# Moving layer 1's first normalise, transpose and gate into the experts' second round

## The chip, the core and the metric

The kernel runs on one core of one Trainium2 chip. Its time is the device time in microseconds (us) of one execution; each figure given as a median is the median of several executions. The engines of the core are PE (TensorE, matrix products and transposes), DVE (VectorE), ACT (ScalarE), POOL (GpSimd) and SP (SyncE, which here only issues transfers). They run their own instruction queues in order and meet at semaphores.

## What is computed

The reference is a network of two layers over x of shape (2, 2048, 256). Cut to what matters here:

```
x = L0_attn_x
xn = layernorm(x)
s = linear_attention(xn)                     # layer 0
g = silu(block(xn))                          # softmax attention + mixture of 8 experts, top 2
x = x + s * g
xn = layernorm(x)                            # layer 1
s = softmax_attention(xn; Wq, Wk, Wv, Wo)    # 16 heads of 32, causal per 2048 tokens
g = silu(xn @ int4(kernel) + bias + (xn @ a) @ b)
x = x + s * g
```

The tokens lie in 32 tiles of 128, 16 tiles for each of the two batches. Layer 1 needs the finished `x` of layer 0, and so the output of the experts for each token.

## The kernel before, in words

**Layer 0's attention** runs first and ends at about 1443 us of the profile. What follows has two stages, and the change touches both and the border between them.

**The experts** (the loops over `h` and `e` from L1356 on). Each expert's 1024 slots are done in two rounds of 512: `h` = 0 for all eight experts, then `h` = 1. One pass of the inner loop loads the expert's weights, biases and slots (`xe`), transposes `xe` on PE (L1374), applies the norm's scale on DVE (`affine`, L1322), makes the hidden layer with 16 matmuls and a Gelu on ACT (L1380, L1381), then the output with 32 matmuls (L1386), adds the bias on DVE (`ye`, L1389) and writes `ye` to `slots_out` (L1391). This stage is written out in program order and a framework's scheduler places each engine's instructions.

Two generators advance between experts. `int4` (L1269) rounds the gate's weight `wl` to int4. `first_mix` is `early_mix` (L1327): for the first four tiles (tokens whose slots all lie in the first round) it gathers the experts' rows from `slots_out` (POOL, L1337), weighs and adds them (L1344 to L1346), applies the Silu (ACT, L1348), multiplies by `s` and adds x (L1349, L1350), and takes the norm's statistics (`norms`). It is advanced from the third expert of the second round on (L1394).

**Layer 1's attention** is written as steps on a list. `Plan` orders all steps of all engines with a search over a model of their costs, and the order that it finds is what each engine runs. `run_attention` (L529) first adds the parts that `prepare` (L1727) returns for the first head group, then interleaves two passes over blocks of the score matrix: pass a takes row maxima (L554 on PE, L567 and L573 on DVE), pass b forms the weights (L587, L1585, L520 on PE, the exponential L599 on ACT), sums them (POOL, L1597 to L1602) and multiplies by the values (L1620, L1631).

The parts for batch 0 go in chunks `c` of four tiles:
- `mix(n0)` for the tiles that `early_mix` has not done: load x and s (L1451, L1452), gather (POOL, L1459), weigh (ACT, L1468), add (DVE, L1473, L1474), Silu (ACT, L1439), multiply and add (L1481, L1482), statistics (DVE L491, L493; POOL L477 and its neighbours);
- `norm(G, t)` for two tiles: scale (ACT, L1501 into `hn`), transpose (PE, L372), copy to `xt` (ACT, L1508);
- `project`: queries and keys of the chunk (PE L1527, copies L1532 on ACT and L1534 on DVE) and values (PE L1542, copy L1548);
- `gate(0, c)`: the low-rank product (PE L1698, copied to `lt` by DVE at L1703), twelve matmuls with `wl` and `lb` (PE L1713, L1714), Silu (ACT L1720), and two writes to `g_dram` (SP, L1725), which `finish` reads at L1682.

`parts.insert` in `prepare` sets the order of these parts before the search. PSUM has eight banks in this stage, five `s` and two `t` banks in the experts' stage; `turn_pair` there takes a `t` bank.

Of the kernel before, what the change touches and what calls it, by code (L numbers as in the profile page):

```python
# [10 lines left out]
F32 = mybir.dt.float32  # L11
# [315 lines left out]
def kernel(ctx: ExitStack, tc: tile.TileContext, i: dict, out: bass.AP):  # L327
# [9 lines left out]
    def bank(tag="s"):  # L337
        return psum[0].tile([P, 512], F32, tag=tag, name=tag, bufs={"s": 5, "t": 2, "av": 1}[tag])
# [126 lines left out]
    def slots(pool, name, count, shape, dt=F32):  # L465
        return [
            lambda n=n: pool.tile(list(shape), dt, tag=f"{name}{n}", name=name, bufs=1) for n in range(count)
        ]
# [203 lines left out]
    with ExitStack() as sc:  # L672
# [70 lines left out]
        def norm(G, t):  # L743
            hn, tp = Buf("hn"), Buf("s")
            n0 = G.b * NT + t

            def shrink():
                for n in range(2):
                    nc.scalar.mul(hn.t[:, n], xr[:, n0 + n], ln_r1[:, n0 + n : n0 + n + 1])

            def scale():
                for k in range(2):
                    nc.vector.tensor_scalar(
                        ht[:, k, t * P : (t + 2) * P], tp.t[:, 2 * k * P : 2 * (k + 1) * P],
                        cols[:, k : k + 1], cols[:, 2 + k : 3 + k], ALU.mult, ALU.add,
                    )

            S("prep", "ACT", 0.75, shrink, r=[("xr", n0), ("xr", n0 + 1), r_of[n0]], w=[hn])
            S("prep", "PE", 0.45, lambda: turn_pair((hn.t[:, 0], hn.t[:, 1]), tp.t), r=[hn], w=[tp])
            S("prep", "DVE", 0.9, scale, r=[tp], w=[("ht", t), ("ht", t + 1)])  # L760
# [503 lines left out]
    for mpad in mpads1:  # L1264
        nc.gpsimd.memset(mpad, 0.0)
    lt = w.tile([17, 512], F32, name="lt")
    nc.gpsimd.memset(lt, 1.0)

    def int4_grid(pool):  # L1269
# [47 lines left out]
    with ExitStack() as sc:  # L1317
        wk = sc.enter_context(tc.tile_pool(name="moe", bufs=2))
        int4 = int4_grid(sc.enter_context(tc.tile_pool(name="int4", bufs=1)))

        def affine(dst, src, k):
            nc.vector.tensor_scalar(dst, src, cols[:, 4 + k : 5 + k], cols[:, 6 + k : 7 + k], ALU.mult, ALU.add)  # L1322

        after = mybir.DependencyInfo(mybir.DependencyClass.Sync, mybir.DependencyReason.DATA)
        w1_in = i["L0_ffn_W1"].rearrange("e (k p) f -> e p k f", p=P)
        w2_in = i["L0_ffn_W2"].rearrange("e (f p) n -> e p f n", p=P)
        def early_mix(n0, pool):  # L1327

            gx, xs = (pool.tile([P, 2, 4, D], F32, name=x) for x in ("early_g", "early_x"))
            x = xr[:, n0 : n0 + 4]
            nc.sync.dma_start(xs[:, 0], x_in[:, n0 : n0 + 4])
            nc.sync.dma_start(xs[:, 1], s_dram[:, n0 : n0 + 4])
            for n, (_, back, _) in enumerate(routes):
                for t in range(4):
                    nc.gpsimd.indirect_dma_start(  # L1337
                        out=gx[:, n, t], out_offset=None, in_=slots_out[: E * HALF],
                        in_offset=bass.IndirectOffsetOnAxis(ap=back[:, n0 + t : n0 + t + 1], axis=0),
                    )  # L1340
            yield
            for n, (_, _, m) in enumerate(routes):
                for t in range(4):
                    nc.vector.tensor_scalar_mul(gx[:, n, t], gx[:, n, t], m[:, n0 + t : n0 + t + 1])  # L1344
            nc.vector.tensor_tensor(gx[:, 0], gx[:, 0], gx[:, 1], ALU.add)
            nc.vector.tensor_tensor(gx[:, 0], gx[:, 0], x, ALU.add)  # L1346
            yield
            nc.scalar.activation(gx[:, 0], gx[:, 0], AF.Silu)  # L1348
            nc.vector.tensor_tensor(gx[:, 0], gx[:, 0], xs[:, 1], ALU.mult)  # L1349
            nc.vector.tensor_tensor(x, gx[:, 0], xs[:, 0], ALU.add)  # L1350
            yield
            norms(pool, lambda strand, eng, cost, fn, **_: fn())("", n0, "", ln_r, ln_m)

        first_mix = early_mix(0, sc.enter_context(tc.tile_pool(name="early", bufs=1)))

        for h in range(2):  # L1356
            for e in range(E):
                w1, w2 = carried[e % 2].rearrange("p (k f) -> p k f", k=2), carried[2 + e % 2].rearrange("p (f n) -> p f n", n=D)
                nc.sync.dma_start(w1, w1_in[e])
                nc.sync.dma_start(w2, w2_in[e])  # L1360
                b2 = wk.tile([P, D], F32, name="b2")
                nc.sync.dma_start(b2, i["L0_ffn_b2"][e : e + 1, :].to_broadcast([P, D]))
                r0 = e * CAP + h * HALF
                xe = wk.tile([P, 4, D], F32, name="xe")
                load = nc.sync.dma_start(xe, slots_in[r0 : r0 + HALF, :].rearrange("(s p) d -> p s d", p=P))
                for inst in sent if e == h == 0 else ():
                    tc.add_manual_dep(load.ins, inst.name, after, reason="every token is in its place")
                if e == h == 0:
                    load_l1()
                xt = wk.tile([P, 2, 512], F32, name="xt")  # L1370
                for k in range(2):
                    tp = bank("t")
                    for s in range(4):
                        nc.tensor.transpose(tp[:, s * P : (s + 1) * P], xe[:, s, k * P : (k + 1) * P], ident)  # L1374
                    affine(xt[:, k], tp, k)
                hm = wk.tile([P, FF // P, 512], F32, name="hm")
                for f in range(FF // P):
                    ps = bank()
                    for k in range(2):
                        nc.tensor.matmul(ps, w1[:, k, f * P : (f + 1) * P], xt[:, k], start=k == 0, stop=k == 1)  # L1380
                    nc.scalar.activation(hm[:, f], ps, AF.Gelu, bias=b1c[:, e * 8 + f : e * 8 + f + 1])  # L1381
                ye = wk.tile([P, 4, D], F32, name="ye")
                for s in range(4):
                    ps = bank()
                    for f in range(FF // P):
                        nc.tensor.matmul(  # L1386
                            ps[:, :D], hm[:, f, s * P : (s + 1) * P], w2[:, f], start=f == 0, stop=f == FF // P - 1
                        )
                    nc.vector.tensor_tensor(ye[:, s], ps[:, :D], b2, ALU.add)  # L1389
                out0 = (h * E + e) * HALF  # L1390
                nc.sync.dma_start(slots_out[out0 : out0 + HALF, :].rearrange("(s p) d -> p s d", p=P), ye)  # L1391
                if e or h:
                    next(int4, None)
                if h and e > 1:  # L1394
                    next(first_mix, None)
        for _ in int4:
            pass
    ps_moe.close()


# [1 line left out]

    g_dram = dram.tile([P, NA, D], F32, name="g_dram")
    with ExitStack() as sc:
        wk = sc.enter_context(tc.tile_pool(name="l1", bufs=2))
        ps = sc.enter_context(tc.tile_pool(name="ps_l1", bufs=1, space=bass.MemoryType.PSUM))
# [3 lines left out]
                **held, vt=slots(wk, "vt", 2, [P, NT, 4, 32]),  # L1412
                mx=slots(wk, "mx", 2, [P, 2, 4, 4]), pt=slots(wk, "pt", 5, [P, 4, 512]), ps=slots(wk, "ps", 2, [P, 4, QC]),
                hn=slots(w, "hn", 1, [P, 2, D]), wg=slots(w, "wg", 1, [P, 3, 2, P]),
                xt=slots(w, "xt", 1, [P, 2, T]), m=slots(wk, "m", 2, [P, 2, 4]),
                mhalf=slots(wk, "mhalf", 2, [P, 2, 2, 4], BF16), mh=slots(wk, "mh", 3, [P, 512], BF16),
                un=slots(wk, "un", 3, [P, 512]), oc=slots(wk, "oc", 2, [P, QC]),
                rs=slots(wk, "rs", 2, [P, 8, 1]), rw=slots(wk, "rw", 1, [P, 8, 32]),
# [12 lines left out]
        def mix(n0, of=2):  # L1431

            both = [(n0 + n, Buf("gx"), Buf("xs")) for n in range(0, of, 2)]
            for n0, gx, xs in both:
                fetched(n0, gx, xs)

            def silus():
                for _, gx, _ in both:
                    nc.scalar.activation(gx.t[:, 0], gx.t[:, 0], AF.Silu)  # L1439

            got = [gx for _, gx, _ in both]
            S("mix", "ACT", 1.4 + 0.6 * len(both), silus, r=got, w=got)
            for n0, gx, xs in both:
                mixed(n0, gx, xs)
# [282 lines left out]
        def prepare(G):  # L1727
            parts = []
            project(G, parts)
            if G.g == 0:  # L1730
                for c in range(NT // 4):
                    for t in (0, 2):
                        parts.insert(5 * c + t // 2, lambda t=4 * c + t: norm(G, t))
            if G.b == G.g == 0:
                for c in range(NT // 4):
                    for t in (0, 2) if c else ():
                        parts.insert(8 * c - 2 + t // 2, lambda n0=4 * c + t: mix(n0))
                    parts.insert(8 * c + 2, lambda c=c: gate(0, c))
            return parts

        others = [(24 + 16 * n, lambda n0=NT + 4 * n: mix(n0, 4)) for n in range(NT // 4)]
# [33 lines left out]
```

## Time and profile before

| what | value |
|---|---|
| median of 3 runs | 3442.45 us (3442.42 to 3448.39) |
| the profiled execution | 3434.15 us, span 3432.4 us from first to last instruction |
| last expert's last bias add ends | about 1920.3 us |
| PE busy, first round of experts (1443 to 1676 us) | 229.67 of 233 us |
| PE busy, second round (1676 to 1920 us) | 232.58 of 244 us |
| PE busy, 1920 to 2010 us | 79.61 of 90 us, mean granted clock 0.87 |
| PE busy, 2100 to 2450 us | 338.18 of 350 us |
| PE busy, 2450 to 3325 us | 867.99 of 875 us |
| PE busy, 3325 to 3432 us | 95.86 of 107 us |

Times inside the execution are counted from the start of the span. The rows of PE come from the profile's windows: the busy time of each engine in a stretch, and the mean clock that the throttle granted to TensorE there (1.00 is full speed). A matmul at half clock counts as busy for its whole, longer time, so a full row is not yet a fast one.

### The profile page before, as it was taken

How to read it: one execution, taken by the hardware profiler on the slowest of the kernel's cores; microseconds unless marked ns; L12 is line 12 of the kernel's file. 1: busy time of each engine (PE TensorE's matmuls, PEld its weight loads, DVE VectorE, ACT ScalarE, POOL GpSimd, SP SyncE). 2: the span in 40 equal slices, each digit the busy share in tenths (PEclk: the TensorE clock that was granted, in tenths of full speed). 3: DMA queues.
4: the chain of work that ended last, by engine and by line, in shares of the span. 5: the costliest groups of instructions: out<-in, count | busy, mean ns of one | idle time of the engine just before them, and what ended most of it. 6: DMA issues, size and time to landing. Idle time of an engine off the chain costs nothing.

```text
span 3432.4 us, 84330 instructions
## 1 busy us (share of the span) xinstructions
PE 3313.2 (97%) x35894; PEld 2327.2 (68%) x35894; DVE 2077.7 (61%) x4066; ACT 1669.1 (49%) x3330; POOL 1661.2 (48%) x2239
## 2 busy tenths in 40 slices
PE   6999999999999999799999999999999999999998
PEld 4667777776777777566666566666676666767675
DVE  5777676777676767511211377676766566666674
ACT  3565555655555555311211364655454545554554
POOL 6452232335232223300100268898786667787876
PEclk8999999999999999899999899999999999999998
DMA  5000000000000010233333211110000100000000
GB/s 183 2 2 2 8 8 8 17 23 29 8 11 2 8 39 31 90 115 115 101 115 97 73 45 52 55 45 15 14 16 26 38 29 13 22 14 19 14 26 23
DMA packets 99514, 133.21 MB, mean 39 GB/s; under 512 B 9395, under 2 KB 76671, under 8 KB 99138
## 3 DMA queue, kind: packets, MB, share of 16 engines
q1 hardware_dynamic: 92994, 113.95, 10.5%
q0 software_dynamic: 6144, 13.88, 1.3%
q8 instruction: 281, 4.60, 0.6%
q14 instruction: 95, 0.78, 0.1%
HBM read 92.96 MB, written 37.75 MB: 38 GB/s over the span
## 4 chain that ended last, share of the span: by engine, by line
PE 78%; POOL 11%; DVE 4%; issue 3%; ACT 2%; DMA 1%; SPq 0%; POOLq 0%; DVEq 0%; ACTq 0%
PE banks L554 14%; PE banks L587 13%; PE banks L838 7%; PE s L1386 6%; PE s L1380 6%; PE banks L1620 5%; PE banks L520 4%; PE banks L1527 3%; POOL ps L1601 3%; PE banks L768 3%; POOL ps L1602 2%; POOL ps L1597 2%; PE banks L1585 2%; DVE mx L573 2%; PE banks L1100 2%
## 5 line engine op out<-in xcount | busy, mean ns | idle before, releaser
L599 ACT ACTIVATE pt<-banks 128x512 f32<-128x512 f32 (+1 forms) x2304 | 1164.0, 575 | 705.3 <-PE banks L1585 206.0
L573 DVE TENSOR_REDUCE mx<-banks 128x2 f32<-128x1024 f32 (+3 forms) x1024 | 1121.2, 1122 | 330.6 <-PE banks L587 138.4
L554 PE MATMUL banks<-carried,carried 32*128 32x512 f32 (+3 forms) x5120 | 1232.5, 558 | 12.9 <-DVE mx L573 6.1
L587 PE MATMUL banks<-carried,carried 32*128 32x256 f32 (+1 forms) x9216 | 1236.9, 388 | 1.8 <-DVE mx L573 1.5
L587 PEld LDWEIGHTS banks<-carried,carried 32*128 32x128 f32 x9216 | 925.3, 185 | 34.4 <-DVE mx L573 5.2
L554 PEld LDWEIGHTS banks<-carried,carried 32*128 32x128 f32 x5120 | 483.9, 184 | 205.9 <-issue 108.8
L1597 POOL TENSOR_TENSOR ps<-pt 128x1024 f32<-128x1024 f32 (+1 forms) x159 | 342.8, 2156 | 146.4 <-ACT pt L599 120.4
L1601 POOL TENSOR_TENSOR ps<-ps,pt 128x1024 f32<-128x1024 f32 x127 | 301.0, 2370 | 68.6 <-ACT pt L599 64.0
L775 POOL TENSOR_TENSOR ra<-raw,rope 128x128 f32<-128x128 f32 x128 | 60.0, 469 | 550.5 <-ACT raw L787 473.0
L1585 PE MATMUL banks<-mh,ones_h 3*128 3x512 bf16 (+1 forms) x1152 | 293.4, 369 | 0.2 <-ACT mh L1578 0.2
L567 DVE CUSTOM_DVE_ANT_0 banks<-banks,causal 128x384 f32<-128x384 f32 (+3 forms) x512 | 242.3, 514 | 63.1 <-PE banks L554 55.7
L1602 POOL TENSOR_TENSOR ps<-ps,pt 128x1024 f32<-128x1024 f32 (+1 forms) x127 | 267.8, 2109 | 10.0
L1620 PE MATMUL banks<-pt,vt 128*32 128x256 f32 (+1 forms) x4608 | 269.6, 372 | 2.7 <-ACT pt L599 2.3
L838 PE MATMUL banks<-pt,vt 128*32 128x256 f32 (+1 forms) x4608 | 268.2, 371 | 1.9 <-DVE mx L573 1.4
L1389 DVE TENSOR_TENSOR ye<-s,b 128x256 f32<-128x256 f32 x64 | 27.2, 425 | 384.9 <-PE s L1386 384.9
L1381 ACT ACTIVATE hm<-s,b1c 128x512 f32<-128x512 f32 x128 | 87.9, 687 | 351.4 <-PE s L1380 351.4
L1386 PE MATMUL s<-carried,hm 128*128 128x256 f32 x1024 | 226.2, 382 | 7.5 <-ACT hm L1381 7.5
L1380 PE MATMUL s<-xt,carried 128*128 128x512 f32 x512 | 224.9, 597 | 7.1 <-DVE xt L1322 7.0
L1620 PEld LDWEIGHTS banks<-pt,vt 128*32 128x32 f32 x4608 | 133.8, 110 | 139.7 <-ACT pt L599 42.3
L1386 PEld LDWEIGHTS s<-carried,hm 128*128 128x128 f32 x1024 | 196.1, 192 | 41.8 <-ACT hm L1381 7.9
L520 PEld LDWEIGHTS <-ident_h 32*128 32x128 bf16 x4096 | 200.0, 93 | 29.0 <-issue 13.9
L838 PEld LDWEIGHTS banks<-pt,vt 128*32 128x32 f32 x4608 | 133.3, 109 | 117.3 <-issue 14.9
(273 smaller groups left out, 4163.7 us busy)
## 6 DMA issues: line engine op xcount, KB each, us to landing
carried<-in_L_ffn_W_dram SPq DMA_DIRECT2D x32, 1024.0 KB, 5.9
gl<-g_dram SPq DMA_DIRECT2D x64, 256.0 KB, 2.8
slots_in<-zero SPq DMA_DIRECT2D x8, 1024.0 KB, 10.7
xe<-slots_in SPq DMA_DIRECT2D x16, 512.0 KB, 7.4
slots_out<-ye SPq DMA_DIRECT2D x16, 512.0 KB, 6.9
s_dram<-lo SPq DMA_DIRECT2D x16, 256.0 KB, 2.0
hn<-in_L_attn_x_dram SPq DMA_DIRECT2D x16, 256.0 KB, 2.7
g_dram<-gs SPq DMA_DIRECT2D x16, 256.0 KB, 2.1
```

Of the source, the lines that this page charges most:

```text
L520: nc.tensor.matmul(out, ident_h[r, q], mask[r, q], start=False, stop=q == 3)
L554: nc.tensor.matmul(s.t[:, x, :w], g.qt.t[r, t * P : (t + 1) * P], g.kt.t[r, 512 * k : 512 * k + w], start=True, stop=not (diagonal and cau ...
L573: S("A", "DVE", t_dve(2 * w), lambda: nc.vector.tensor_reduce(mx.t[:, t % 2, i : i + 2, k], s.t[:, :, :w], AX.X, ALU.max), r=[(s, 0), (s, ...
L587: nc.tensor.matmul(s.t[:, at], g.kt.t[r, kj * P : (kj + 1) * P], g.qt.t[r, QC * c + q0 : QC * (c + 1)], start=n == 0, stop=n == 1 and not ...
L599: S("B", "ACT", t_act(w), lambda: nc.scalar.activation(pt.t[:, j, :w], s.t[:, :w], AF.Exp, scale=0.25), r=[s], w=[(pt, j)])
L838: nc.tensor.matmul(av.t[32 * j : 32 * j + 32, q0:QC], vts[G.vn][:, kj, j], pt.t[:, j, at], start=n == 0, stop=n == len(tiles) - 1,)
L1380: nc.tensor.matmul(ps, w1[:, k, f * P : (f + 1) * P], xt[:, k], start=k == 0, stop=k == 1)
L1386: nc.tensor.matmul(ps[:, :D], hm[:, f, s * P : (s + 1) * P], w2[:, f], start=f == 0, stop=f == FF // P - 1)
L1585: return lambda: nc.tensor.matmul(s.t[:, :w_], ones_h[r], G.mh[c].t[r, 512 - w_ :], start=False, stop=last)
L1597: nc.gpsimd.tensor_tensor(ps.t[:, :, q0:], pt.t[:, :, same], pt.t[:, :, odd], ALU.add)
L1601: nc.gpsimd.tensor_tensor(ps.t, ps.t, pt.t[:, :, even], ALU.add)
L1620: nc.tensor.matmul(av.t[32 * j : 32 * j + 32, q0:QC], G.vt.t[:, kj, j], pt.t[:, j, at], start=n == 0, stop=False)
```

## The change

`early_mix` gets two more stages: one that normalises its four tiles, transposes them and copies them to `xt1` (allocated with layer 1's weights; layer 1's `xt` now is this tile), and one that computes the gate of the four tiles and writes it to `g_dram` in one transfer. It starts one expert earlier, so that its stages fall on experts 1 to 6 of the second round (after e = 1, 2, 3, 4: as before; after e = 5 the transposes, after e = 6 the gate); what is left of `int4` is run before the transposes. `prepare` leaves `norm` and `gate` of chunk 0 out and shifts the remaining insertions, so that layer 1's list begins with chunk 0's projection.

```diff
+    xt1 = w.tile([P, 2, T], F32, name="xt1")
+    g_dram = dram.tile([P, NA, D], F32, name="g_dram")
...
             norms(pool, lambda strand, eng, cost, fn, **_: fn())("", n0, "", ln_r, ln_m)
+            yield
+
+            for n in range(4):
+                at = slice(n0 + n, n0 + n + 1)
+                nc.scalar.activation(gx[:, 1, n], xr[:, n0 + n], AF.Identity, bias=ln_m[:, at], scale=ln_r[:, at])
+            for t in range(0, 4, 2):
+                tp = turn_pair((gx[:, 1, t], gx[:, 1, t + 1]))
+                nc.vector.tensor_copy(xt1[:, :, t * P : (t + 2) * P], tp.rearrange("p (k n) -> p k n", k=2))
+            yield
+            pa = bank()
+            for k in range(2):
+                nc.tensor.matmul(pa[:16], la[:, k], xt1[:, k, :512], start=k == 0, stop=k == 1)
+            nc.vector.tensor_copy(lt[:16], pa[:16])
+            for t in range(0, 4, 2):
+                py = bank()
+                for n in range(2):
+                    v, at = py[:, n * D : (n + 1) * D], slice((t + n) * P, (t + n + 1) * P)
+                    for k in range(2):
+                        nc.tensor.matmul(v, xt1[:, k, at], wl[:, k], start=k == 0, stop=False)
+                    nc.tensor.matmul(v, lt[:, at], lb, start=False, stop=True)
+                nc.scalar.activation(xs[:, 0, t : t + 2], py.rearrange("p (n d) -> p n d", n=2), AF.Silu)
+            nc.sync.dma_start(g_dram[:, n0 : n0 + 4], xs[:, 0])
...
-                if h and e > 1:
+                if h and e == 5:
+                    for _ in int4:
+                        pass
+                if h and e:
                     next(first_mix, None)
-        for _ in int4:
-            pass
...
-                xt=slots(w, "xt", 1, [P, 2, T]), m=slots(wk, "m", 2, [P, 2, 4]),
+                xt=[lambda: xt1], m=slots(wk, "m", 2, [P, 2, 4]),
...
-                    for t in (0, 2):
-                        parts.insert(5 * c + t // 2, lambda t=4 * c + t: norm(G, t))
+                    for t in (0, 2) if c or G.b else ():
+                        parts.insert(5 * c + t // 2 - 2 * (1 - G.b), lambda t=4 * c + t: norm(G, t))
...
-                        parts.insert(8 * c - 2 + t // 2, lambda n0=4 * c + t: mix(n0))
-                    parts.insert(8 * c + 2, lambda c=c: gate(0, c))
+                        parts.insert(8 * c - 5 + t // 2, lambda n0=4 * c + t: mix(n0))
+                    if c:
+                        parts.insert(8 * c - 1, lambda c=c: gate(0, c))
```

Because the step list of layer 1 changes, the planner's search gives another order for the whole of layer 1, not only for its beginning.

## The prediction, made before the run

> **What bounds the kernel now.** I read the page's first lines, then the windows of PE around the border between experts and layer 1, then the chain of waits there.
>
> ```profile
> span 3432.4 us, 84330 instructions
> PE 3313.2 (97%) x35894; PEld 2327.2 (68%) x35894; DVE 2077.7 (61%) x4066; ACT 1669.1 (49%) x3330; POOL 1661.2 (48%) x2239
> ```
>
> PE is the bound: 97% busy, 119 us idle in all. A change that only moves PE work can gain idle time and time at a low clock, nothing else. The windows show where both lie (columns: stretch, its length, busy time of PE, PEld, DVE, ACT, POOL, granted clock, DMA share, GB/s):
>
> ```profile
> 1920.30:1924.00 3.70, 1.58 (x9) 0.92 (x9) 0.01 (x1) 2.16 (x4) 0.00 (x0) 0.92 0.40 142
> 1924.00:1931.00 7.00, 6.85 (x24) 3.92 (x24) 0.41 (x1) 1.42 (x3) 5.07 (x6) 0.80 0.71 225
> 1931.00:1933.10 2.10, 0.00 (x0) 0.03 (x1) 1.58 (x3) 1.96 (x3) 1.80 (x2) 1.00 0.35 92
> 1933.10:1940.70 7.60, 7.13 (x24) 2.19 (x24) 4.82 (x16) 3.75 (x8) 1.20 (x2) 0.76 0.37 115
> 1940.70:1953.40 12.70, 12.70 (x30) 7.32 (x31) 5.14 (x21) 0.60 (x1) 7.49 (x17) 0.50 0.25 83
> 1958.70:1960.50 1.80, 0.02 (x1) 0.00 (x0) 0.57 (x3) 1.79 (x6) 0.85 (x5) 1.00 0.01 2
> ```
>
> Idle gaps of 2 us are each followed by a stretch at clock 0.50, and chunk 0's gate runs in the longest one. The chain of waits says what the border waits for (start, us, what):
>
> ```profile
> 1919.88 0.44 DVE ye L1389
> ...
> 1924.41 1.19 POOL gx L1459
> ...
> 1932.41 4.30 DMA gx<-slots_out,back
> 1936.73 0.52 ACT gx L1468
> ...
> 1940.81 2.00 PE banks L1713 x4
> 1942.81 1.15 PE banks L1714 x2
> ...
> 1955.89 0.59 ACT xt L1508
> ...
> 1960.56 5.40 PE banks L1527 x8
> ```
>
> The last expert's rows must be written before the gathers of chunk 1 can start (1924.41, 4.1 us after the experts' end at 1920.3). Eight gathers at 1.25 us, a landing, weighing, Silu, statistics and norm follow before chunk 1 can be projected at 1960.56: **a chain of 40.3 us that starts with the end of the experts.** PE fills it with chunk 0: turns, projection, scores, gate.
>
> **The change, part by part.** Times t below count from the experts' end. Order of instructions is that of the two built programs, read side by side.
>
> *Start one expert earlier; ACT's four scales.* Gathers, weighing and early Silu keep their places in all queues, so PE's 7.5 us wait for that Silu in the second round (PE idle 1696.2 to 1703.7) stays. Four scales of 0.55 us replace two on ACT after 1709.9; the next Gelu is due at 1719.2: nothing. The rest of int4 stood early on DVE already: nothing.
>
> *Turns after expert 5.* PE gets 8 transposes, 1.04 us by L1374's row (x8). They take both `t` banks, so expert 6's transposes wait for the two DVE copies. Step by step from the end of expert 5: ye add to 0.43, copies (0.69 each, row L1637's kind) to 2.1, expert 6's second four transposes to 2.75, first `affine` to 3.0, matmuls at 3.1; before they started 1.5 after (1715.60 to 1717.10). **+1.6 us**, between 1.0 (no bank wait) and 2.5.
>
> *Gate after expert 6.* The price of a gate at full clock stands in the chain at 2004 to 2016:
>
> ```profile
> 2004.23 1.82 PE banks L1698 x4
> ...
> 2009.75 0.86 PE banks L1713 x4
> 2010.61 0.62 PE banks L1714 x2
> 2011.24 1.06 PE banks L1713 x4
> 2012.30 0.62 PE banks L1714 x2
> ```
>
> 1.82 + 4 x (1.06 + 0.62) = 8.5 us. The copy to `lt` (0.68) lies beside the first L1713 pair. PE has nothing else meanwhile: **+8.5 us**. ACT gets two Silus (0.60 each) and two table loads (1.28 each); the first load is ahead of the products, the second delays expert 7's first Gelu by 1.3 us, covered because five `s` banks let PE run ahead and Gelus take 0.69 of every 1.73 us. Without that cover: 1.3. SP's single g_dram write stands ahead of the last two experts' `slots_out`: it is issued about 20 us before the last one is ready: nothing; if it held that write, every us would be one on the chain. Stage total: **+10.1 us**, and this moves the start of the chain.
>
> *What is taken out of layer 1.* 8 transposes, the gate (3.50 us at L1698's cold rate plus 12.2 from 1940.81 to 1952.99), the ACT scales and copies. On PE that is some 17 us, but it was filler. How much sooner is chunk 1 projected? PE projects chunk 0 at full clock from t = 0 (3.5 us, then values 1.95: done at 5.5). The copy of the queries stands on ACT behind four weighings, as before (1931.54, t = 11.2), that of the keys behind L1474 on DVE, so the scores start at t = 12.8, as before (1933.1). **PE idles 7.3 us there, where it idled 2.1.** Gathers, landing and weighing end at 17.9 (before 18.2); adds 18.6, Silu 19.3; DVE has only five L567 ahead of the mix (before ten, 1939.15 to 1942.9), so statistics end at 23.2 (before 25.6); POOL's roots, 3.1 us, at 26.4. Now the gain: in the trace the scales waited from 1949.2 to 1953.95 because the gate's two Silus stood before them on ACT, waiting for PE at half clock. Without them: scales 27.5, turn 28.2, copy 28.9, scales 29.9, turn 30.6, `mh` copy between, copy 31.2. PE has pass b's start ahead of the projection (2.6 us by 1956.05 to 1958.7, from `mh` at 30.6): chunk 1 at **t = 33.7 instead of 40.3: -6.6 us**.
>
> *Afterwards.* Both orders do the same PE work up to chunk 2's values (211 queue rows from projection to projection's end in both), and PE is nearly full there. Chunk 2's gathers start at t = 28.3 instead of 29.3, so that chain gains only 1 us while PE wants it 6.6 sooner: its keys' copy stands on DVE behind adds that wait for these gathers. I take 0.5 us; between 0 (slack as in the trace, 3.7 us of idle from 1966 to 2000) and 5.
>
> **Sum:** 10.1 - 6.6 + 0.5 = **+4.0 us**. Profiled execution 3434.15 -> 3438.2; the median of the runs shown stands 8.3 above that execution, so 3442.45 + 4.0 = **3446.5 us**.
>
> *A rule against the change.* The row first: after the 2.1 us gap PE ran 12.7 us at clock 0.50 although it was busy throughout. The Trainium skill, page "TensorE: Matmul & The Clock Gate", Part 1, says the clock is halved after an idle window of about 3.4 us and comes back after one busy window. By it, a 7.3 us gap surely costs half rate, but only some 3.4 us of it, 1.7 us of work; by the row it can last four windows. In my sum the projection keeps the trace's 5.40 us (3.5 at full clock), so one cold stretch is in it; four windows would add up to 4.7 us. I take the first, as little dense work falls into the stretch, and keep the second for the range. The trace agrees with the rule on the halving, not on its length.
>
> **Rivals.**
> - *A, the trade as summed (+4.0, spread 0 to +8), 55%.* The border is bound by the chain from the last `slots_out`, so work taken out of it leaves idle time and is paid in full in the experts.
> - *B, chunk 2 is late too, 25%.* ACT has chunk 1's gate Silus ahead of chunk 2's scales in the new order (in the old one behind). If PE reaches chunk 2 with its norm not done, the 5 us above and a longer cold stretch come in: +4 + 5 + 2 = +11, 3453.5. For it: only 1 us is gained at the gathers. Against: the new order puts chunk 2's turns further back on PE. It decides once chunk 2's turns wait more than 3 us.
> - *C, the other sign, 12%: the gate's half clock is the real loss.* If the gathers start at 3.1 (when SP's loads start, 1923.43) and PE stays warm, the projection comes at 32 and the later gates run at full clock, saving the 3.5 us of idle from 1966 to 2000: 10.1 - 8.3 - 3.5 - 4 (cold time of projection and scores) = -6, 3436.5. Against: the 7.3 us gap.
> - *D, the redrawn order decides, 8%.* 12 us of PE idle at 2100 to 2450 and 11 after 3325 depend on the search; either may move by 5 to 8 both ways, without a sign.
>
> About 0.2% (6.9 us) is what a measurement of this kernel can tell from no change. Of A some two thirds stays within, the rest is slower (0.36, 0.19); B is slower but for 0.04; C gives 0.05 faster, 0.07 same; D 0.02, 0.04, 0.02. Faster 0.07, same 0.51, slower 0.42. The range leaves a tenth out at each end: 3440 to 3456.
>
> **What would show it.** Experts' second round longer by 9 to 11 us, ending near 1930.4; PE idle near 7 us between chunk 0's values and the first scores, clock 0.50 after it; chunk 1's projection at about 1964 (1960.56 before); ACT's scales of chunk 1 right behind POOL's roots. I am wrong if the gate in the experts costs under 7 us, if chunk 1 comes before 1958, or if PE's idle after 2010 differs by more than 5 us.

## The result and the profile after

| | before | after |
|---|---|---|
| median | 3442.95 us (4 runs, 3442.42 to 3448.39) | 3465.23 us (4 runs, 3464.57 to 3468.44) |
| profiled execution | 3434.15 us, span 3432.4 | 3465.79 us, span 3463.7 |
| experts, first transpose to last bias add | 478.64 us | 489.33 us |
| from there to chunk 1's projection | 40.3 us | 32.9 us |
| from there to the end | 1471.8 us | 1492.0 us |

The ratio is 1.0068 (95% interval 1.0052 to 1.0085): 22 us slower, where 4 were forecast and 3456 us was the upper end. The two spans differ by more, 31.3 us. Of this 7.8 lies before the experts start (1449.46 against 1441.68 us), in layer 0's attention, which the change does not touch; there PE is busy 7.7 us longer with the same matmuls. The execution of before that was profiled is some 9 us below the median in the table. The other three rows are the result: +10.7, -7.4, +20.2.

The page after begins so:

```profile
span 3463.7 us, 84331 instructions
PE 3326.7 (96%) x35894; PEld 2333.0 (67%) x35894; DVE 2077.8 (60%) x4068; ACT 1668.9 (48%) x3330; POOL 1662.6 (48%) x2239
```

PE is 13.5 us longer busy with the same number of matmuls, and it is idle for 137 us instead of 119. By stage, its busy time is 7.7 us longer in layer 0's attention, 10.0 longer in the experts, which now do the moved work, and only 4.3 shorter in layer 1, which no longer does it (1465.3 against 1469.6). Nearly all the new idle time, 17.2 us, lies in layer 1. The first two of the three rows are read in the windows of PE (stretch, length, busy time of PE, PEld, DVE, ACT, POOL, granted clock, DMA share, GB/s):

```profile
1900.40:1909.00 8.60, 8.60 (x30) 4.23 (x30) 1.10 (x2) 0.60 (x1) 0.00 (x0) 1.00 0.17 61
1938.80:1944.30 5.50, 5.48 (x24) 3.38 (x24) 0.00 (x0) 0.00 (x0) 1.22 (x2) 1.00 0.50 174
1944.30:1951.50 7.20, 0.01 (x1) 0.00 (x0) 2.04 (x3) 3.34 (x6) 5.68 (x6) 0.80 0.61 194
1951.50:1954.10 2.60, 2.57 (x16) 1.47 (x16) 1.56 (x3) 2.45 (x6) 1.05 (x2) 0.50 0.35 102
1960.00:1971.60 11.60, 8.97 (x52) 6.30 (x53) 5.32 (x21) 6.07 (x11) 8.53 (x19) 0.50 0.28 86
```

The first row is the gate in the experts: PE busy throughout, at full clock, with nothing but the gate to do. The second and third are chunk 0's projection, at once, and the gap of 7.2 us after it. The fourth and fifth are at clock 0.50. The chain of waits over the same border:

```profile
1942.78 1.19 POOL gx L1483
...
1951.91 2.63 DMA gx<-slots_out,back
1954.57 0.52 ACT gx L1492
...
1960.48 1.06 POOL ln_r L477
...
1963.28 0.61 ACT hn L1525
...
1966.99 0.90 PE banks L372 x3
...
1971.67 3.65 PE banks L1551 x7
```

It is the chain of before without its last detour: ACT's scales (L1525) start the moment POOL has finished the roots. Up to here the trade is as summed. What remains is layer 1 after the border, where 0.5 us was forecast and 20 came.

### The profile page after: what moved, and what is told of

Its sections match the earlier page's. It is cut to its first block, busy times and chain, and to the rows that moved or that the text cites. A ratio compares the mean times of both kernels' runs of the same rounds, so it can differ in the third digit from the quotient of the medians.

```text
span 3463.7 us, 84331 instructions
## 1 busy us (share of the span) xinstructions
PE 3326.7 (96%) x35894; PEld 2333.0 (67%) x35894; DVE 2077.8 (60%) x4068; ACT 1668.9 (48%) x3330; POOL 1662.6 (48%) x2239
## 3 DMA queue, kind: packets, MB, share of 16 engines
q1 hardware_dynamic: 92850, 113.95, 10.1%
## 4 chain that ended last, share of the span: by engine, by line
PE 77%; POOL 12%; DVE 4%; issue 3%; ACT 2%; DMA 1%; POOLq 0%; SPq 0%; DVEq 0%; ACTq 0%
PE banks L554 14%; PE banks L587 12%; PE banks L838 7%; PE s L1410 6%; PE s L1404 6%; PE banks L1644 5%; PE banks L520 4%; POOL ps L1625 3%; PE banks L768 3%; PE banks L1551 2%; POOL ps L1626 2%; POOL ps L1621 2%; PE banks L1609 2%; DVE mx L573 2%; PE banks L1100 2%
## 5 line engine op out<-in xcount | busy, mean ns | idle before, releaser
L554 PE MATMUL banks<-carried,carried 32*128 32x512 f32 (+3 forms) x5120 | 1245.3, 562 | 23.1 <-DVE mx L573 8.0
```

Source lines behind the costliest of these rows:

```text
L554: nc.tensor.matmul(s.t[:, x, :w], g.qt.t[r, t * P : (t + 1) * P], g.kt.t[r, 512 * k : 512 * k + w], start=True, stop=not (diagonal and cau ...
```

## The experiments

Two theories of the 20 us. **D: the redrawn order.** The plan's search draws random handicaps; with three parts fewer it finds another order for the whole of layer 1, and that order is slower on the chip. **S: the shorter cover.** With the gate gone, PE is starved at the border, and mix, norm and the later gates stay late whatever the order. Each kernel was compared with runs of the kernel before on its own chip. The three groups of four ran on three chips; on the one of seeds 2 and 3 the kernel before takes 3489.4 us (3439.3 and 3441.2 on the others), so only ratios are compared. The us given with a ratio are worked out from it; it is not simply the quotient of the two medians, so their difference can be another number.

### The experts' extra work alone

```diff
+            for t in range(0, 4, 2):
+                tp = turn_pair((gx[:, 1, t], gx[:, 1, t + 1]))
+                nc.vector.tensor_copy(xtd[:, :, t * P : (t + 2) * P], tp.rearrange("p (k n) -> p k n", k=2))
+            yield
+            pa = bank()
+            for k in range(2):
+                nc.tensor.matmul(pa[:16], la[:, k], xtd[:, k, :512], start=k == 0, stop=k == 1)
...
+            nc.sync.dma_start(g_spare[:, n0 : n0 + 4], xs[:, 0])
```

> The kernel before, with the four tiles' scales, turns and gate done a second time, early in the experts' second round, into tensors that nobody reads; layer 1 keeps its own copy of that work, its list and its order. Extra work, the output is the reference's. If the loss of the change splits as the two profiles say (experts' stage +10.7, the rest in layer 1), this kernel is slower than before by 10 to 12 us (ratio about 1.0032) and its experts' stage takes 489 us instead of 478.6, with layer 1 as before. If instead the early work also disturbs layer 1 (a later start of the gathers, a colder PE), it is slower by 15 to 22 us. If the gate hides in the experts, it is slower by under 5.

Measured: 3449.71 us, ratio 1.0028 (1.0009 to 1.0047), which is 9.6 us (3 to 16). The experts' price is paid, and no further loss can be told. (The profiled execution has 490.7 us in the experts, 12.0 more than before, and puts layer 1 at 1505.6 us, 6.5 shorter than before with the same order; see the last section.)

### Layer 1's new order alone

```diff
-                tp = turn_pair((gx[:, 1, t], gx[:, 1, t + 1]))
-                nc.vector.tensor_copy(xt1[:, :, t * P : (t + 2) * P], tp.rearrange("p (k n) -> p k n", k=2))
...
-            nc.sync.dma_start(g_dram[:, n0 : n0 + 4], xs[:, 0])
+            for k in range(2):
+                nc.gpsimd.tensor_copy(xt1[:, k, :512], xr[:, n0 + 2 * k : n0 + 2 * k + 2].rearrange("p n d -> p (n d)"))
+            nc.sync.dma_start(g_dram[:, n0 : n0 + 4], gx[:, 0])
```

> The changed kernel without the early work: scales, turns and gate of the first four tiles are left out of the experts and of layer 1 (stand-in data is copied in their place), so layer 1 has exactly the changed list and order. It has some 17 us of TensorE work less than the kernel before. Theory 1 (layer 1 itself loses, by its cover and its order): about 11 to 13 us slower than before although the work is left out. Theory 2 (layer 1 would gain its 6 us, and only the early work in the experts makes it late): 5 to 7 us faster than before.

The kernel leaves out the four tiles' scales, turns and gate; stand-in data is copied in their place, so layer 1 runs the changed kernel's instructions on wrong values. Measured: 3452.3 us, ratio 1.0046 (1.0031 to 1.0060): 16 us **slower** with some 9.5 us of PE work taken out (its length at full clock: 8.5 for the gate and 1.04 for the turns). So the loss in layer 1 does not come from what the experts do; with the run above it adds up to the change (0.28 + 0.46 against 0.68%). It does not tell the order from the cover, since both are in it.

### The search with other seeds

```diff
-        draw = random.Random(0)
+        draw = random.Random(self.SEED)
```

`SEED` is 1, 2 or 3 in layer 1; layer 0 keeps 0.

> The kernel before with layer 1's order drawn from another seed. Theory D (orders of equal cost in the planner differ by ten us or more on the chip, and before has a lucky one): 8 to 15 us slower than before. Theory S: within 4 us of before.

> The changed kernel with layer 1's order drawn by the search from another seed. Theory D (the drawn order is an unlucky one): 8 to 15 us faster than the changed kernel, near 3450 to 3457. Theory S (the shorter cover makes the loss whatever the order): within 4 us of the changed kernel, 3461 to 3469.

> The kernel before, layer 1's order drawn from a third seed. Theory D (the kernel before owns a lucky draw; a usual draw is 10 to 16 us slower): 3449 to 3456, and 8 to 12 us faster than the changed kernel of the same seed. Theory S (the change makes layer 1 some 13 us longer whatever the draw): within 5 us of the kernel before, and some 24 us faster than the changed kernel of the same seed.

> The changed kernel, layer 1's order drawn from the third seed. Theory D: 8 to 12 us slower than the kernel before with this seed, which is the price of the experts' stage alone. Theory S: some 24 us slower than it, near 3463.

> The kernel before, fourth seed. Theory D: 3449 to 3456. Theory S: within 5 us of the kernel before.

> The changed kernel, fourth seed. Theory D: 8 to 12 us slower than the kernel before with this seed. Theory S: some 24 us slower than it.

Ratios to the kernel before (95% interval), and the span that the plan itself works out for layer 1 with its cost model:

| seed | before's steps | plan's span | changed steps | plan's span |
|---|---|---|---|---|
| 0 | 1 | 1520.29 | 1.0068 (1.0052 to 1.0085) | 1519.45 |
| 1 | 1.0069 (1.0043 to 1.0095) | 1520.73 | 1.0083 (1.0056 to 1.0109) | 1522.16 |
| 2 | 1.0075 (1.0055 to 1.0096) | 1521.33 | 1.0035 (1.0020 to 1.0050) | 1520.16 |
| 3 | 1.0136 (1.0112 to 1.0160) | 1522.45 | 1.0079 (1.0060 to 1.0099) | 1520.11 |

One number, the seed, costs the kernel before 0.7 to 1.4%, as much as the whole change or twice that. With seeds 2 and 3 the change is even a gain. The plan tells its orders apart by 3 us, the chip by 47, and it put the changed steps 0.84 us below those of before. So of eight draws the one of the kernel before is the fastest, and the change gave it away. (With the experts' 0.28% taken off, the changed kernel with seed 2 comes to 1.0007, which cannot be told from it; the other six stay slower.) Neither theory had this in full: D expected a changed kernel 8 to 12 us slower than before at each seed, S some 24; it is +5, -14 and -20 us (differences of the ratios, each uncertain by some 10 us). Taken alone, the changed kernel with seed 1 came out as S had it (3466 us), and the kernel before with seed 1 lost 24 us, more than D had allowed.

### The whole change in the old order

The list of parts in the changed kernel is that of before with `norm(0)`, `norm(2)` and `gate(0, 0)` taken out; the rest stands in the same sequence. So if those steps stay in the plan and issue nothing, the search sees what it saw before and every engine keeps its order.

```diff
+            done = G.b == 0 and t < 4
+            S("prep", "ACT", 0.75, (lambda: None) if done else scale, r=[("xr", n0), ("xr", n0 + 1), ("r", n0 // 4 * 4)], w=[hn])
+            S("prep", "PE", 0.45, lambda: done or turn_pair((hn.t[:, 0], hn.t[:, 1]), tp.t), r=[hn], w=[tp, (xt, "claim")])
...
+            if b == c == 0:
+                S = lambda strand, eng, cost, fn, **k: plan.step(strand, eng, cost, lambda: None, **k)
```

The `parts.insert` lines are those of before.

> The whole change (scales, turns and gate of the first four tiles in the experts' second round), but layer 1 keeps the list and the drawn order of the kernel before on every engine: the moved steps stand in the plan and issue nothing. Theory D (the loss of 20 us in layer 1 comes from the redrawn order): experts +10.7, chunk 1's projection some 4 to 8 us sooner, nothing afterwards: 2 to 8 us slower than before (ratio 1.0006 to 1.0023). Theory S (a shorter cover makes layer 1 late whatever the order): 18 to 26 us slower (1.0052 to 1.0075).

Measured: 3446.31 us against 3441.16, ratio 1.0022 (1.0013 to 1.0030): 7.5 us slower. The plan's span is again the 1520.29 of before. This kernel and the changed one do the same work from the same list, and differ in the drawn order alone; the intervals do not touch. **16 of the 23 us are the order** (0.68 - 0.22% of 3441; some 9 to 22 us with both intervals). The changed kernel itself did not run on this chip, so this compares two ratios. The profiles say the same without them: from chunk 1's projection to the end it is 1466.9 to 1471.9 us in all six executions profiled in the old order, and 1492.1 and 1490.7 us in the two in the new one (the changed kernel and the one that leaves the early work out). Theory S falls: with the border bare, as in the changed kernel (a gap of 7.2 us after chunk 0's projection, chunk 1 projected 34.5 us after the experts), nothing is lost afterwards.

What does the slower order lack? The windows of the second, third and fourth 100 us of layer 1, first of the changed kernel, then of this one:

```profile
2038.80:2138.80 100.00, 95.18 (x978) 61.28 (x973) 65.89 (x113) 48.91 (x92) 72.39 (x59) 0.99 0.15 50
2138.80:2238.80 100.00, 93.11 (x1095) 64.96 (x1091) 65.11 (x144) 54.28 (x105) 89.95 (x90) 0.98 0.07 22
2238.80:2338.80 100.00, 92.41 (x1094) 62.18 (x1094) 71.96 (x123) 54.66 (x107) 89.96 (x77) 1.00 0.17 54
```

```profile
2037.20:2137.20 100.00, 97.06 (x1029) 62.56 (x1025) 72.18 (x120) 51.32 (x99) 80.52 (x69) 0.98 0.14 45
2137.20:2237.20 100.00, 97.16 (x1148) 67.57 (x1146) 65.22 (x144) 55.19 (x105) 88.47 (x87) 1.00 0.15 45
2237.20:2337.20 100.00, 95.06 (x1020) 65.05 (x1016) 75.88 (x122) 56.31 (x109) 91.55 (x76) 0.93 0.14 43
```

PE is idle 19.3 us in the three rows of the first and 10.7 in those of the second. POOL's column points to a place: in the first 100 us it does 8 us less (72 against 81), and in the next 200 it is some 90% busy in both, so it does not catch up. One group of PE with what ended its idle time, of the changed kernel, of this one and of the kernel before (busy, mean ns, idle before, releasers):

```profile
L1595 PE MATMUL banks<-cst,mpad 128*128 128x128 f32 x128 | 27.1, 294 | 16.0 <-POOL mpad L1591 15.3 <-ACT pt L599 0.5
```

```profile
L1596 PE MATMUL banks<-cst,mpad 128*128 128x128 f32 x128 | 26.9, 292 | 8.9 <-POOL mpad L1592 6.4 <-DVE mx L567 1.9
```

```profile
L1571 PE MATMUL banks<-cst,mpad 128*128 128x128 f32 x128 | 26.6, 290 | 6.7 <-POOL mpad L1567 6.3
```

`mpad` is the row maximum in three pieces, six small POOL instructions that PE needs for pass b. In the changed kernel PE waits 15.3 us for them, 10.7 of that between 2038 and 2340; in the old order 6.4, and 2.1 in the same stretch. One such wait in the timeline of the changed kernel (start, us, engine, line, operation, in brackets the idle time before):

```profile
2172.82 0.95 POOL L1483 DMA_INDIRECT gx<-slots_out,back  x1 [0.30 <-issue]
2174.07 0.95 POOL L1483 DMA_INDIRECT gx<-slots_out,back  x1 [0.30 <-issue]
2175.32 0.94 POOL L1483 DMA_INDIRECT gx<-slots_out,back  x1 [0.30 <-issue]
2176.27 0.20 POOL L1589 CAST mhalf<-m 128x8 bf16<-128x8 f32 x1
...
2178.39 0.21 POOL L1591 TENSOR_TENSOR mpad<-m,mpad 128x8 f32<-128x8 f32 x1
2178.65 0.44 PE L1595 MATMUL banks<-cst,mpad 128*128 128x128 f32 x2 [2.65 <-POOL mpad L1591]
```

The maximum that the pieces start from was ready at 2173.64 (DVE's L1597), but five gathers at 1.25 us were drawn ahead of the pieces on POOL, which began them 2.6 us later; PE stood for 2.65. All eight waits between 2038 and 2340 are of this kind: the maximum was ready 2.1 to 6.5 us before POOL came to it. But gathers stand right ahead in two of the eight only (4.2 of the 10.7 us), in the others it is sums; and in the old order seven gathers stand ahead of the pieces once (2232.8 to 2241.4), and PE waits 0.80 there. What the waits share is that POOL comes late to the pieces, not what it does before them.

These waits are a part of the loss. The profiled executions of the two kernels differ in layer 1 by 23.5 us (1524.9 against 1501.4; that of the old order is 5.8 below its median). PE is idle 9.4 us longer (59.6 against 50.2), of which the `mpad` waits make 8.9, and busy 14.2 us longer with the same 16916 matmuls. Of this 7.1 is a lower clock (26.0 against 18.9; the busy time multiplied by one minus the granted clock, window by window). The other 7 are not accounted for. Nor are the `mpad` waits what makes a draw slow in general. The kernel before with seed 2 has hardly any, and it is 0.75% slower:

```profile
L1572 PE MATMUL banks<-cst,mpad 128*128 128x128 f32 x128 | 26.5, 291 | 3.1 <-POOL mpad L1568 2.2 <-ACT pt L600 0.5
```

That the order costs the time is shown; by which of its waits it does so is read from one profile, and no step was moved alone.

### Turns alone

> Scales and turns alone in the experts, the gate stays at its place in layer 1, in the order of the kernel before. The experts pay 1.6 to 2.3 us, the border keeps the gate as its cover. Theory D: within 3 us of before. Theory S: if the early turns alone upset layer 1, over 5 us slower; if only the missing gate does, within 3 us of before as well.

The edit is the one above without the gate's part: `gate(0, 0)` stays a step of layer 1. Measured: 3445.05 us, ratio 1.0010 (0.9997 to 1.0023). The experts take 480.0 us, 1.4 more than before. There is no gain at the border: chunk 1 is projected 42.6 us after the experts (40.3 before), with the gate cold again.

### The early Silu behind its Gelus

The prediction noted a stall that the change leaves in place: PE waits 7.5 us in the second round because the scheduler put the early Silu into ACT's queue ahead of the Gelu that PE needs, before its data were there. An edge keeps it behind the Gelus of the expert after which it is written:

```diff
-            nc.scalar.activation(gx[:, 0], gx[:, 0], AF.Silu)
+            early = nc.scalar.activation(gx[:, 0], gx[:, 0], AF.Silu)
+            tc.add_manual_dep(early.ins, gelus[-1], mybir.DependencyInfo(mybir.DependencyClass.NoSync, mybir.DependencyReason.DATA), reason="behind this expert's Gelu")
```

> The kernel before, with one edge more: the early Silu in the experts' second round stands behind the Gelus of the expert after which it is written, so that TensorE no longer waits 7.5 us for it (1696.2 to 1703.7). Layer 1 is untouched. If that stall is on the path: 6 to 8.5 us faster than before (ratio 0.9975 to 0.9983). If the throttle or another wait gives it back: within 3 us.

> The two edits together: turns alone in the experts with the order of the kernel before, and the Silu behind its expert's Gelus. If they add: the sum of the two before it, 4 to 9 us faster than before.

Measured: 3432.86 us, ratio 0.9980 (0.9971 to 0.9989), and with the turns moved as well 3432.69, ratio 0.9979 (0.9969 to 0.9988). Both beat both kernels; the turns add nothing that can be told. The wait of PE in the kernel before (in total, times, longest) and the window that follows it, then the same group and the window of the experts' stage in the kernel with the edge alone:

```profile
PE s L1386 <- ACT hm L1381: 7.5, 1, 7.5
1703.70:1708.00 4.30, 4.30 (x10) 3.49 (x11) 2.57 (x10) 0.00 (x0) 1.18 (x2) 0.50 0.02 6
```

```profile
L1389 PE MATMUL s<-carried,hm 128*128 128x256 f32 x1024 | 223.6, 379 | 0.0
```

```profile
1446.50:1915.20 468.70, 461.09 (x1664) 306.55 (x1664) 73.03 (x152) 93.71 (x134) 10.76 (x17) 1.00 0.33 106
```

The wait is gone, and the stage is 9.9 us shorter (478.64 before), not 7.5: PE is also busy 2.5 us less with the same matmuls (463.57 before), about what the cold stretch after the stall had cost (4.3 us at 0.50).

## Why the prediction was wrong

- **Experts +10.1: right.** Measured +10.7 in the profiles, +9.6 when done alone. Over all profiles the stage takes 478.6 to 480.7 us in five executions without the early work and 488.5 to 490.8 in six with all of it. The gate took 8.6 us at full clock with nothing else for PE to do (8.5 forecast). The turns took 1.4 when moved alone and 2.6 with the Silu moved too (471.2 against 468.6); 1.6 was forecast, and a stage that varies by 2 us cannot tell these apart.
- **Border -6.6: right for this profile, and by some luck.** Chunk 1 is projected 32.9 us after the experts' end (33.7 forecast), the gap on PE is 7.2 us (7.3), the clock after it 0.50, and the scales stand right behind POOL's roots. Two errors cancel: the scales start at 24.5 us (27.5 forecast), and from there to the projection it takes 8.4 us (6.2 forecast). And the 40.3 us that the gain was counted from are those of an execution in which chunk 0's gate ran cold. In an execution with the gate in its old place at full clock it is 33.7 us (last section), and against that the change gains next to nothing at the border.
- **The rule of the clock gate, weighed there** (the Trainium skill, "TensorE: Matmul & The Clock Gate", Part 1): after the 7.2 us gap the clock stayed at 0.50 from 1951.5 to 1971.6. This is no test of the rule's one busy window of about 3.4 us, since PE kept pausing: before 1966.5 its longest unbroken stretch was 3.35 us. The row of before was misread as well. The 12.7 us at 0.50 did not follow on the 2.1 us gap: between them the clock was at 0.50 from 1934 to 1937 and back at 1.00 from 1938 to 1940. So the gap was followed by 3 us at half clock, though it is shorter than the rule's idle window; and what set off the 12.7 us, busy throughout and longer than the rule's busy window, stays open. The choice between the rule and the row did not decide the outcome: in the first 50 us of layer 1 the time lost at low clock is 8.8 us after and 10.3 before.
- **"Afterwards: both orders do the same PE work up to chunk 2's values ... I take 0.5 us": wrong, it was +20.2.** The step compared the two orders up to there and took what follows as the same. It was not: the plan had redrawn the rest of layer 1. In that draw PE's idle time after the first 90 us of layer 1 is 45.4 us instead of 32.4 (the sign named for being wrong was 5); 9.0 of the 13 are longer waits for POOL's `mpad`. In the old order the change comes to +7.5 us (4.5 to 10.3), where the sum said +4.0.
- **Rival D named the cause and had its size wrong:** "either may move by 5 to 8 both ways", with a chance of 8%. It measured 16 us here, and 24 to 47 for another seed of the kernel before. "Without a sign" did not hold either: none of the seven other draws is faster. Its range was taken from two idle stretches of 12 and 11 us. Counted from the experts' end they grew to 21.8 and 14.4, which is 13 us together, and the longer busy time (14.2 us against the old order) had no place in it.
- **Rival B** (chunk 2's norm late, +11) is not what happened: PE's waits for the scales (L372 on `hn`, L1525) are 1.7 us in all after and 1.4 before. **Rival C** (gain by a warm gate) fell with the gap, as argued, but its premise holds: the gate's half clock is what the border lost in the profile of before. Theory S, formed on the result, fell with the old order's run.

## What to carry to other kernels

When a schedule comes out of a search, an edit to its steps has two prices: that of the edit, and that of a new draw. Before costing the first, ask what the second can be (another seed with nothing else changed measures it), and separate the two by leaving the removed steps in the plan with nothing in them. A kernel that was kept because it was fast is likely to hold a good draw, so that the second price is more often a loss than a gain; here seven draws out of seven were no faster, which is one kernel's evidence.

## What the runs showed of the hardware

The same order of matmuls does not get the same clock in each execution. In the kernel before, chunk 0's gate ran at 0.50 for 12.7 us with PE busy throughout, and its matmuls with `wl` took 634 ns at the median. In the kernel with the experts' extra work alone, whose layer 1 has the same order, the same sixteen took 379 ns. Its first row here is the tile's (min, median, max in ns), the others are windows:

```profile
L1740 PE MATMUL banks<-wl,xt x16: 379/379/484, 1960.1 to 1965.9; 128*128 128x256 f32 x16
```

```profile
1954.10:1961.70 7.60, 7.59 (x30) 3.20 (x30) 6.32 (x23) 3.70 (x8) 1.22 (x3) 0.78 0.36 104
1961.70:1974.40 12.70, 10.32 (x77) 6.86 (x76) 7.65 (x27) 6.80 (x13) 8.49 (x18) 1.00 0.35 115
```

Counted from the experts' end, these are the stretches that the prediction showed at 0.76 and 0.50: the second ran at full clock this time. The scales, which wait behind the gate's Silus, start at 27.3 us instead of 33.6, and chunk 1 is projected at 33.7 us instead of 40.3:

```profile
1974.99 1.29 PE L1554 MATMUL banks<-xt,wg 128*128 128x512 f32 x2 [1.93 <-ACT xt L1535]
```

From there to the end it is 1471.9 us (1471.8 before), so layer 1 is shorter by these 6.5 us and by nothing else; without moving anything they are nearly what the change gained at the border (7.4). Of the five profiles with this gate in the old order three have it cold (634 ns) and two warm (379). A cold stretch of one profile is therefore no fixed cost of the place where it stands; single executions of the kernel before lay up to 23 us apart on one chip (3429.55 to 3452.7 us).
